# Moving one statistics instruction, a chunk's fusion and a norm's last step within the period of an attention-and-Mamba kernel

## The chip, the cores and the metric

The kernel runs on one core of a Trainium2 chip. The metric is the device time of one execution in microseconds, taken as the median of several runs. The engines are named as in the profile: PE (TensorE), DVE (VectorE), ACT (ScalarE), POOL (GpSimd) and SP (SyncE, which issues the DMAs). [...]

## The reference

The input x is 8 samples of 512 channels by 48 x 48 = 2304 positions. Two layers are applied, each with a residual:

```
x = x + attention(group_norm(x))      # causal linear attention, 8 heads of 64
x = x + mamba_groups(group_norm(x))   # 4 groups of 128 channels, one after the other
```

The attention projects q, k and v (512 x 512 each), takes elu + 1 of q and k, and forms for each position the causal sum of k v^T, read with q and divided by the running sum of k. The second layer splits the 512 channels in four. For each group i a Mamba block runs over the 2304 positions: in-projection, a causal convolution of width 4, silu, softplus of a step size, a scan h = dA * h + dBu with 256 channels x 16 states, a weighted sum over the states, a gate silu(z), an out-projection. Its output x_m is fused with its input x_i:

```
fused = sigmoid(mean(x_i)) * x_i + sigmoid(mean(max(x_i, x_m))) * max(x_i, x_m)
x_(i+1) = normed group i+1 + fused
```

so that a group's Mamba block needs the fusion of the group before. The group norms have 32 groups of 16 channels and use the mean and the variance over all positions.

## The kernel before, in words

Positions are cut into 6 chunks of LC = 384. A **job** is one chunk of one Mamba block: 192 jobs in all, of two interleaved streams (even and odd samples). A job is 8 **slots**. A slot multiplies and scans two pairs of states: one product on DVE (L809), a smaller one on POOL (L798), four exponentials dA = exp(delta * A) on ACT (L819, each into one of six PSUM banks), four scans on DVE (L830), one multiplication by C on POOL (L846), and four matmuls on PE that sum over the states (L853) into the bank `yp`. The exponentials are issued three ahead of the scans (DEPTH), five ahead just before silu and softplus (L670 and L704), because those two need another table on ACT and come back with a second table load.

Everything else is fitted in beside the slots. Each slot has two **halves**: `beside(2 * k)` is called before its first scan, `beside(2 * k + 1)` after its second. At each half a planner goes through its tasks and lets each one issue its next step once the step's due half is reached (`when[0]`), a least distance to its last step has passed (`when[1]`), and the banks that it wants are free. The tasks are written by hand as generators that yield their due halves:

- `chunk` (L266) computes one chunk of attention, started 16 halves after the one before it; its times are `at(j)`, j halves after its start. At `at(24)` DVE adds the attention's output to x (`xr`, L450), and `bn_stats` (L452) takes the chunk's statistics for the second layer's norm. After the sixth chunk `group_norm` (L162) makes the norm in five steps: aggregation and a matmul, three small DVE operations (L174 to L178), a second matmul, `pow` on POOL (L191, preceded by L188 on DVE), and two small DVE operations that use its result (L195).
- `prepare` (L623) makes a job's inputs before its first half `first`: convolution matmuls (L635) at first - 21 and first - 19, four silu on ACT (L671 to L676) at first - 18, then the step size, softplus (L706) four halves on, and the DMAs that spread rows over partitions.
- `pass_on` (L524) hands one block to the next: for each chunk c it loads three tiles by SP (L569, L572, L574), scales two or three of them on ACT (L596, L597 and L601, or L607 where a new sample starts), and adds on POOL (L604 and L609 one half apart, and L612 for the output). `self.ready` then lets the job's convolution start. Chunk 0 runs as soon as the block before is done; chunks 1 to 5 have due halves relative to their job's `first`.

In steady state `first` is a multiple of 16 and a chunk of attention starts 13 halves before it, so that everything repeats with a **period** of 16 halves, which holds one job and one chunk of attention. Below, "half n" is a half's number modulo 16, with half 0 at a job's first scan:

| step | half |
|---|---|
| attention output and its statistics (L450, L452) | 11 |
| convolutions (L635) | 11, 13 |
| silu (L671 to L676) | 14 |
| softplus (L706) | 2 |
| loads of a chunk's fusion, c = 1 to 5 | 12 |
| its scaling on ACT; its three additions on POOL | 2; 3, 4, 5 |
| scaling on ACT of chunk 0; its additions | 8; 9, 10, 11 |
| norm after a sixth chunk: five steps | 15, 0, 1, 2, 3 |
| exponentials for k on ACT (L298, L299); k on DVE (L351) | 6; 7 |

Of the kernel before, what the change touches and what calls it, by code (L numbers as in the profile page):

```python
# [49 lines left out]
def attention_then_mamba_kernel(  # L50
# [18 lines left out]
    B, _, L = x.shape  # L69
# [84 lines left out]
    def save(out, in_):  # L154
        stores.append((half_no[0], out, in_))

    def flush(every=True):
        while stores and (every or stores[0][0] <= half_no[0] - 2):
            _, o, i = stores.pop(0)
            nc.sync.dma_start(out=o, in_=i)  # L160
# [46 lines left out]
    norms, xns, x1s, done, ksums = {}, {}, {}, {}, {}  # L207
# [58 lines left out]
    def chunk(m):  # L266


        b, o, c = parts[m]
# [3 lines left out]
        cols, tile_rows = slice(c * LC, (c + 1) * LC), slice(o * P, (o + 1) * P)  # L273
# [6 lines left out]
        def new(tag, bufs=1, shape=(P, LC)):  # L280
            return apool.tile(list(shape), F32, tag=tag, name=f"{tag}_{n}", bufs=bufs)
# [50 lines left out]
        S, stats, ksum = passes[b, o]  # L332
# [90 lines left out]
        xr = new("xr")  # L423
# [25 lines left out]
        yield at(24), 0  # L449
        nc.vector.tensor_add(xr, xr, ops)  # L450
        bank.free()
        nc.vector.bn_stats(stats[:, 0, c, :], xr)  # L452
        save(x1s[b][tile_rows, cols], xr)
        if c + 1 == NC:
            norm = yield from group_norm(
                stats, 1, f"m{b}_{o}", 8, [(times[m] + j, 1) for j in (28, 29, 29, 30, 31)]
            )
            flush()
            done[b, o] = norm

    class Stream:
# [62 lines left out]
        def pass_on(self):  # L524


            xi = self.xi
            old = None
            if self.b is not None:
                old = self.b, self.s, self.n, self.fm  # L530
                wt = small.tile([P, 4], F32, tag="wt", name=f"wt_{self.n}")
                nc.vector.tensor_copy(wt[:, 2:3], self.sums)
                nc.vector.tensor_reduce(wt[:, 3:4], self.fsum, AX.X, ALU.add)
            last = old is not None and old[1] == 3 and not self.samples
            if not last:
                self.move_on()
                while (self.b, self.s) not in done:
                    yield "1w", 0
                norm = done[self.b, self.s]
            s = self.s  # L540
            if old is not None:
                yield "1", 0

                nc.scalar.activation(wt[:, 0:2], wt[:, 2:4], AF.Exp, scale=-1.0 / L)
                yield "1", 0
                nc.vector.tensor_scalar_add(wt[:, 0:2], wt[:, 0:2], 1.0)
                nc.vector.reciprocal(wt[:, 0:2], wt[:, 0:2])
            else:
                yield "1", 0
            if not last:  # L550
                if self.fresh:
                    self.sums = norm[:, 2, :]
                else:

                    sums = small.tile([P, 2], F32, tag="sums", name=f"sums_{self.n}", bufs=3)
                    nc.vector.tensor_scalar(
                        sums[:, 0:1], wt[:, 2:3], wt[:, 0:1], norm[:, 2, :], ALU.mult, ALU.add
                    )
                    nc.vector.tensor_scalar(
                        sums[:, 1:2], wt[:, 3:4], wt[:, 1:2], sums[:, 0:1], ALU.mult, ALU.add  # L560
                    )
                    self.sums = sums[:, 1:2]

            def loads(c):
                fu = xb = xa = None
                cols = slice(c * LC, (c + 1) * LC)
                if not last:
                    xb = mpool.tile([P, LC], F32, tag="xb", name=f"xb_{self.n}_{c}")
                    nc.sync.dma_start(out=xb, in_=x1s[self.b][s * P : (s + 1) * P, cols])  # L569
                if old is not None:  # L570
                    fu = mpool.tile([P, LC], F32, tag="fu", name=f"fu_{old[2]}_{c}")
                    nc.sync.dma_start(out=fu, in_=old[3][:, cols])  # L572
                    xa = mpool.tile([P, LC], F32, tag="xo", name=f"xo_{old[2]}_{c}")
                    nc.sync.dma_start(out=xa, in_=x1s[old[0]][old[1] * P : (old[1] + 1) * P, cols])  # L574
                return fu, xb, xa

            now = loads(0)
            for c in range(NC):

                if c and not last:  # L580
                    first = 2 * self.jobs[self.block * NC + c].start
                    yield (first - 36, 1), 0
                    now = loads(c)
                    yield (first - 30, 1), 0
                elif c:
                    yield "3", 0
                    now = loads(c)
                    yield "1", 0
                else:
                    yield "1", 0  # L590
                cols, icols = slice(c * LC, (c + 1) * LC), slice(3 + c * LC, 3 + (c + 1) * LC)
                fu, xb, xa = now
                if not last:
                    normed = dict(bias=norm[:, 1, :], scale=norm[:, 0, :])
                if old is not None:
                    nc.scalar.activation(fu, fu, AF.Copy, scale=wt[:, 1:2])  # L596
                    nc.scalar.activation(xi[:, icols], xi[:, icols], AF.Copy, scale=wt[:, 0:1])  # L597
                if old is None:
                    nc.scalar.activation(xi[:, icols], xb, AF.Identity, **normed)
                elif not last and not self.fresh:  # L600
                    nc.scalar.activation(xb, xb, AF.Identity, **normed)  # L601
                if old is not None:
                    yield "1", 0
                    nc.gpsimd.tensor_tensor(fu, fu, xi[:, icols], ALU.add)  # L604
                    yield "1", 0
                    if not last and self.fresh:
                        nc.scalar.activation(xi[:, icols], xb, AF.Identity, **normed)  # L607
                    elif not last:
                        nc.gpsimd.tensor_tensor(xi[:, icols], xb, fu, ALU.add)  # L609
                    self.ready = c + 1  # L610
                    yield "1", 0
                    nc.gpsimd.tensor_tensor(xa, xa, fu, ALU.add)  # L612
                    save(out[old[0], old[1] * P : (old[1] + 1) * P, cols], xa)
                self.ready = c + 1
# [335 lines left out]
    parts, times = [], []  # L950
# [17 lines left out]
    for b in counted:  # L968
        first = times[parts.index((b, 0, 0))]
        begins[b] = (first - 20) // PERIOD * PERIOD - 4 * NC * PERIOD - 2 if b > 1 else first - 64  # L970

    def begin(latest):

        nonlocal begun, put
        while counted and begins[counted[0]] - 4 <= half_no[0]:
            tasks.append(Task(statistics(counted.pop(0))))
        while put < len(parts) and times[put] - 6 <= half_no[0]:
            put += 1
            heads.append(Task(chunk(put - 1), before=heads[-1] if heads else None))
        while (  # L980
            begun < len(jobs)
            and jobs[begun].start <= latest
            and jobs[begun].stream.block == jobs[begun].block
            and jobs[begun].stream.ready > jobs[begun].c
        ):
            tasks.append(Task(jobs[begun].prepare(), jobs[begun].start))
            begun += 1
# [41 lines left out]
    def at(k):  # L1029
        return jobs[k // SLOTS], k % SLOTS  # L1030
# [170 lines left out]
```

## Time and profile before

| | us |
|---|---|
| median of 3 runs (lowest, highest) | 9154.76 (9140.69, 9157.51) |
| the profiled execution's own time | 9167.14 |
| its span, first to last instruction | 9165.3 |
| DVE busy | 8342.1 |
| POOL busy | 8066.8 |
| PE busy | 7631.5 |
| ACT busy | 6579.4 |

The span is divided by what the engines did; a share of busy time does not say by itself which engine sets the end. In the timelines shown below a line gives the start, the duration, the engine, the source line and operation, the tile written and read, and how many instructions are merged; in brackets stands the idle time of the engine before it and what ended it.

### The profile page before, as it was taken

The page shows a single profiled execution, that of the slowest core. Times are in us where ns is not written, and L with a number is a line of the kernel's source. Part 1 is how long each engine was busy: PE and PEld are TensorE (multiplying, and loading weights), DVE is VectorE, ACT ScalarE, POOL GpSimd, SP SyncE. Part 2 cuts the span into 40 slices and gives each one's busy share as a digit, 9 for nine tenths or more (in the row PEclk, how much of TensorE's full clock was granted, in tenths as well). Part 3 has the DMA queues.
Part 4 walks back from the last instruction along what each step waited for, and adds up shares of the span by engine and source line. Part 5 has one row for each costly group of instructions (what it writes and reads, how often), then busy time and mean ns, then how long its engine had stood idle before and what let it go on. Part 6 is the DMA issues. An engine that isn't in the chain of part 4 may idle for free.

```text
span 9165.3 us, 120476 instructions
## 1 busy us (share of the span) xinstructions
PE 7631.5 (83%) x35714; PEld 3602.8 (39%) x35714; DVE 8342.1 (91%) x11640; ACT 6579.4 (72%) x12656; POOL 8066.8 (88%) x5635
## 2 busy tenths in 40 slices
PE   7888888888888888888888888888888888888865
PEld 4443444433344444443333444444333444444321
DVE  3899999999999999999999999999999999999997
ACT  2677777777777777777777777777777777777775
POOL 1788989899988899899998888998999898989998
PEclk9999999999999999999999999999999999999977
DMA  5566666666766666666666666666666666666654
GB/s 182 161 173 180 185 184 184 181 188 180 196 173 179 184 186 187 183 180 181 191 184 182 174 178 187 187 184 184 180 188 183 181 179 177 178 178 177 164 156 129
DMA packets 1002898, 1642.84 MB, mean 179 GB/s; under 512 B 138592, under 2 KB 797312, under 8 KB 1002240
## 3 DMA queue, kind: packets, MB, share of 16 engines
q1 hardware_dynamic: 1002240, 1635.13, 65.0%
q8 instruction: 283, 4.64, 0.2%
q14 instruction: 375, 3.07, 0.1%
HBM read 1309.06 MB, written 325.58 MB: 178 GB/s over the span
## 4 chain that ended last, share of the span: by engine, by line
DVE 31%; ACT 21%; PE 18%; POOL 10%; DMA 9%; issue 8%; SPq 3%; POOLq 0%; DVEq 0%; ACTq 0%
DVE u L830 20%; ACT bank L819 7%; PE bank L635 6%; POOL u L846 6%; DVE u L809 6%; PE bank L286 5%; ACT L819 4%; PE yp L853 3%; PE bank L646 3%; POOL u L798 2%; DMA C<-scr 2%; ACT L706 2%; ACT bank L299 1%; DMA B<-scr 1%; SPq L739 1%
## 5 line engine op out<-in xcount | busy, mean ns | idle before, releaser
L830 DVE TENSOR_TENSOR_SCAN u<-bank,u 128x385 f32<-128x385 f32 (+1 forms) x6144 | 5471.0, 939 | 378.3 <-ACT bank L819 331.9
L846 POOL TENSOR_TENSOR u<-u,C 128x1536 f32<-128x1536 f32 x1536 | 4880.6, 3177 | 216.4 <-DVE gm_m L175 83.2
L819 ACT ACTIVATE bank<-dr,av 128x385 f32<-128x385 f32 (+1 forms) x6144 | 3432.3, 579 | 1406.9 <-DVE u L830 1118.1
L853 PE MATMUL yp<-u,cst 128*64 128x384 f32 x12288 | 2429.2, 516 | 505.7 <-ACT yp L787 263.9
L798 POOL TENSOR_TENSOR u<-B,dxr 128x512 f32<-128x512 f32 x1536 | 1958.8, 1275 | 21.4 <-DMA dxr<-xscr 16.9
L809 DVE TENSOR_TENSOR u<-B,dxp 128x1024 f32<-128x1024 f32 x1536 | 1835.0, 1195 | 9.4 <-ACT dxp L782 9.4
L286 PE MATMUL bank<-xn,wq_sb 128*128 128x384 f32 x4608 | 1730.3, 520 | 97.1 <-DVE u L830 40.4
L853 PEld LDWEIGHTS yp<-u,cst 128*64 128x64 f32 x12288 | 781.0, 139 | 1713.3 <-issue 1051.6
L635 PE MATMUL bank<-xi,wk 128*128 128x384 f32 x3072 | 1122.1, 509 | 306.1 <-ACT kl L383 234.3
L286 PEld LDWEIGHTS bank<-xn,wq_sb 128*128 128x128 f32 x4608 | 870.0, 199 | 894.6 <-DVE u L830 153.6
L635 PEld LDWEIGHTS bank<-xi,wk 128*128 128x128 f32 x3072 | 563.0, 193 | 878.2 <-ACT kl L383 351.5
L844 POOL COPY state<-u 128x4 f32<-128x4 f32 x1280 | 241.7, 189 | 538.4 <-DVE u L830 522.7
L298 ACT ACTIVATE ex<-bank,bqkv_sb 128x384 f32<-128x384 f32 x384 | 219.6, 572 | 520.1 <-PE bank L286 491.6
L747 POOL TENSOR_TENSOR delta<-delta,xs 128x384 f32<-128x384 f32 x384 | 384.6, 1002 | 141.6 <-DMA dscr<-delta 124.6
L819 ACT ACT_TABLE_LOAD x382 | 490.1, 1283 | 6.7
L787 ACT ACTIVATE yp<-xs,pv 128x384 f32<-128x384 f32 x384 | 222.7, 580 | 373.2 <-DVE yz L865 373.2
L871 PE MATMUL bank<-yz,wo 128*128 128x384 f32 x768 | 307.0, 517 | 55.5 <-DVE yz L865 36.7
L695 PE MATMUL bank<-dbc,wd 9*128 9x384 f32 x768 | 302.2, 513 | 3.2 <-ACT dbc L687 3.2
L646 PE MATMUL bank<-xi,wi 128*128 128x384 f32 x768 | 289.2, 498 | 14.3 <-ACT xs L671 14.3
L416 PE MATMUL bank<-cst,rdb 128*128 128x128 f32 x576 | 103.2, 290 | 228.3 <-DVE u L830 226.1
L447 PE MATMUL bank<-sm,v 128*64 128x128 f32 x2304 | 260.9, 305 | 33.8 <-DVE u L830 30.6
L682 PE MATMUL bank<-xs,wx 128*40 128x384 f32 x768 | 281.3, 489 | 0.8 <-DVE sm L434 0.8
(109 smaller groups left out, 7632.7 us busy)
## 6 DMA issues: line engine op xcount, KB each, us to landing
B<-scr SPq DMA_DIRECT2D x1536, 192.0 KB
C<-scr SPq DMA_DIRECT2D x1536, 192.0 KB
xn<-xn SPq DMA_DIRECT2D x192, 768.0 KB
dr<-dscr SPq DMA_DIRECT2D x768, 192.0 KB
dxr<-xscr SPq DMA_DIRECT2D x768, 192.0 KB
dscr<-delta SPq DMA_DIRECT2D x192, 384.0 KB
xscr<-delta SPq DMA_DIRECT2D x192, 384.0 KB
xn<-in_x SPq DMA_DIRECT2D x48, 768.0 KB
```

The costliest lines, as they stand in the source:

```text
L286: nc.tensor.matmul(ps, wq_sb[:, kt, j * 512 + o * P : j * 512 + (o + 1) * P], xn[:, kt, :], start=(kt == 0), stop=(kt == 3),)
L635: nc.tensor.matmul(xc, wk[:, k, h * P : (h + 1) * P], xi[:, c0 + k : c0 + k + LC], start=(k == 0), stop=(k == 3),)
L646: nc.tensor.matmul(zp, wi[:, 256 + h * P : 256 + (h + 1) * P], xi[:, c0 + 3 : c0 + 3 + LC], start=True, stop=True,)
L695: nc.tensor.matmul(vp, wd[32:41, h * P : (h + 1) * P], dbc[32:41, :], start=True, stop=True)
L747: nc.gpsimd.tensor_tensor(delta[:, h, :], delta[:, h, :], xs[:, h, :], ALU.mult)
L798: nc.gpsimd.tensor_tensor(u[:, :, :, 1 + LC - TAIL :], self.B[s % 4][:, :, cols].unsqueeze(2).to_broadcast(shape), self.dxr[s // 4][:, :, ...
L809: nc.vector.tensor_mul(u[:, :, :, 1 : 1 + LC - TAIL], self.B[s % 4][:, :, cols].unsqueeze(2).to_broadcast(shape), self.dxp.unsqueeze(1).to ...
L819: nc.scalar.activation(dA[:, cols], self.dr[h][:, g, cols], AF.Exp, scale=self.w[6][:, 2 * h + g, q + j : q + j + 1],)
L830: nc.vector.tensor_tensor_scan(u[:, j, g, cols], dA[:, cols], u[:, j, g, cols], 0.0, ALU.mult, ALU.add,)
L846: nc.gpsimd.tensor_tensor(h, h, self.C[s % 4].unsqueeze(2).to_broadcast([P, NG, 2, LC]), ALU.mult)
L853: nc.tensor.matmul(self.yp[g * 64 : g * 64 + 64, 0:LC], pair_sum, u[:, j, g, 1:], start=False, stop=(s % 4 == 3 and j == NG - 1), skip_gro ...
L871: nc.tensor.matmul(self.xm[:, 0:LC], self.w[2][:, h, :], self.yz[:, h, :], start=(h == 0), stop=(h == 1),)
```

## The change

Three steps are moved; no instruction is added or removed.

1. `bn_stats` on the attention's output leaves `at(24)` and gets a step of its own at `at(28)`: half 15 in place of half 11. The norm after a sixth chunk starts one half later than that.
2. The fusion of chunks 1 to 5 is loaded at first - 33 in place of first - 36 and scaled at first - 25 in place of first - 30; the additions follow one, two and three halves after the scaling as before. In halves: loads 12 to 15, ACT 2 to 7, POOL 3, 4, 5 to 8, 9, 10.
3. The due half of the norm's last step is 32 in place of 31. As each step is due at least one half after the one before, the five steps, which were issued at halves 15, 0, 1, 2, 3, are issued at 0, 1, 2, 3, 4.

```diff
         nc.vector.tensor_add(xr, xr, ops)
         bank.free()
+        save(x1s[b][tile_rows, cols], xr)
+        yield at(28), 0
         nc.vector.bn_stats(stats[:, 0, c, :], xr)
-        save(x1s[b][tile_rows, cols], xr)
         if c + 1 == NC:
             norm = yield from group_norm(
-                stats, 1, f"m{b}_{o}", 8, [(times[m] + j, 1) for j in (28, 29, 29, 30, 31)]
+                stats, 1, f"m{b}_{o}", 8, [(times[m] + j, 1) for j in (28, 29, 29, 30, 32)]
             )
...
                 if c and not last:
                     first = 2 * self.jobs[self.block * NC + c].start
-                    yield (first - 36, 1), 0
+                    yield (first - 33, 1), 0
                     now = loads(c)
-                    yield (first - 30, 1), 0
+                    yield (first - 25, 1), 0
                 elif c:
                     yield "3", 0
```

## Prediction

> **What bounds the kernel now.** I read the page first, then DVE's waits, then timelines of single periods.
>
> ```profile
> PE 7631.5 (83%) x35714; PEld 3602.8 (39%) x35714; DVE 8342.1 (91%) x11640; ACT 6579.4 (72%) x12656; POOL 8066.8 (88%) x5635
> L830 DVE TENSOR_TENSOR_SCAN u<-bank,u 128x385 f32<-128x385 f32 (+1 forms) x6144 | 5471.0, 939 | 378.3 <-ACT bank L819 331.9
> ```
>
> DVE is the busiest engine and its scans alone are 5471 us, so the end is set by DVE's work plus its waits, 9165 - 8342 = 823 us. The view of waits says for whom:
>
> ```profile
> DVE u L830 <- ACT bank L819: 331.9, 198, 4.4
> DVE k L351 <- ACT bank L299: 142.0, 135, 5.3
> DVE norm_m L195 <- POOL norm_m L191: 43.4, 31, 2.2
> DVE u L830 <- POOL state L844: 25.0, 70, 0.4
> ```
>
> (total us, times, longest.) I then gave each DVE wait in the timeline its half by counting scans, over the 174 periods of steady state: 270.3 us at half 15 (every period, 1.55 on average), 125.4 at half 7, 48.0 at half 3, 37.4 at half 4, 41 elsewhere. Everywhere else DVE runs without a gap. One period, DVE and then ACT:
>
> ```profile
> 4640.07 0.56 DVE L452 BATCH_NORM_STATS2 stats_m<-xr 128x6 f32<-128x384 f32 x1
> 4640.55 1.78 DVE L830 TENSOR_TENSOR_SCAN u<-bank,u 128x384 f32<-128x384 f32 x2
> ...
> 4651.64 0.95 DVE L830 TENSOR_TENSOR_SCAN u<-bank,u 128x384 f32<-128x384 f32 x1
> 4654.62 2.65 DVE L830 TENSOR_TENSOR_SCAN u<-bank,u 128x384 f32<-128x384 f32 x3 [2.04 <-ACT bank L819]
> ```
> ```profile
> 4649.33 1.28 ACT L671 ACT_TABLE_LOAD   x1
> ...
> 4652.71 1.28 ACT L819 ACT_TABLE_LOAD   x1
> 4654.01 1.09 ACT L819 ACTIVATE bank<-dr,av 128x384 f32<-128x384 f32 x2
> ```
>
> In silu's slot ACT makes no exponential from 4649.33 to 4654.01. DVE uses up the five in hand and stands for 2.04 us. The statistics run at half 11, back to back with scans, fully paid.
>
> The wait at half 7 has a chain behind it (ACT, PE, DVE of another period):
>
> ```profile
> 793.25 0.61 ACT L596 ACTIVATE fu<-fu,wt 128x384 f32<-128x384 f32 x1
> ...
> 794.28 0.69 ACT L601 ACTIVATE xb<-xb,norm_m 128x384 f32<-128x384 f32 x1
> ...
> 801.49 0.57 ACT L787 ACTIVATE yp<-xs,pv 128x384 f32<-128x384 f32 x1
> ```
> ```profile
> 802.21 2.10 PE L853 MATMUL yp<-u,cst 128*64 128x384 f32 x8 [1.99 <-ACT yp L787]
> 804.24 3.91 PE L286 MATMUL bank<-xn,wq_sb 128*128 128x384 f32 x8
> ```
> ```profile
> 809.24 0.55 DVE L351 SCALAR_TENSOR_TENSOR k<-ex,bank 128x384 f32<-128x384 f32 x1 [1.88 <-ACT bank L299]
> ```
>
> The fusion's three scalings stand in ACT's queue just ahead of softplus and its two table loads, and with no gap after them until L787. PE waits 1.99 us for L787, projects k late, and at half speed besides: the same eight matmuls take 2.85 us in a period 90 us earlier, and the granted clock from 804 to 809 is 0.76. ACT's exponential of k and DVE's L351 follow late.
>
> [...] the clock records show 47 episodes at 0.5 of 3.4 us each that begin in half 5. [...]
>
> **The change part by part.** The order of every other step's halves is as before; only the moved ones differ.
>
> *Statistics to half 15.* At half 11, L450 to the scan after L452 is 0.563 + 0.477 us from start to start; an addition followed directly by a scan is 0.46 (L372 to L830). Removal saves 0.58. At half 15 the instruction lies ahead of the waiting scan. ACT's chain there starts from a DVE scan at half 13 and does not depend on it. The trace already has this experiment, since the next sample's own statistics (L239, the same operation on the same shape) fall in this slot in some periods. Median wait with nothing added: 2.03 us (71 periods); with one at half 14: 1.57 (15); one at half 15: 1.35 (15); one at each: 1.07 (42). For example:
>
> ```profile
> 1109.59 0.55 DVE L239 BATCH_NORM_STATS2 stats_a<-xs 128x6 f32<-128x384 f32 x1
> ...
> 1112.12 2.66 DVE L830 TENSOR_TENSOR_SCAN u<-bank,u 128x385 f32<-128x385 f32 x3 [1.12 <-ACT bank L819]
> ```
>
> So it is free while more than about 0.5 us of wait is left, as in all but 3 of 174 periods. Gain 174 x 0.58 = 101 us; if the cover were gone, 174 x 0.1 = 17.
>
> *The norm one half later.* The aggregation (0.22 us to the next instruction) leaves half 15's cover: 29 x 0.22 = 6 lost. `pow` moves on POOL from between L846 and L798 to behind L798:
>
> ```profile
> 889.27 0.54 POOL L191 TENSOR_TENSOR norm_m<-gm_m,power 128x1 f32<-128x1 f32 x1
> 889.78 1.26 POOL L798 TENSOR_TENSOR u<-B,dxr 128x512 f32<-128x512 f32 x1
> ```
> ```profile
> 889.85 0.33 DVE L195 TENSOR_SCALAR norm_m<-gm_m,norm_m 128x1 f32<-128x1 f32 x2 [1.22 <-POOL norm_m L191]
> ```
>
> It will end 1.25 us later, near 891.05. L195 moves behind two scans, a product and the gate: 888.6 + 1.72 + 1.11 + 0.47 = 891.9. The wait disappears with 0.8 us to spare: 29 waits, 41 us; I take 38. The norm must be done by half 5, where `pass_on` asks for it; it is, at half 4.
>
> *The fusion.* ACT loses 0.52 + 0.51 + 0.60 = 1.63 us ahead of softplus. L787 comes at about 799.9, PE's idle time falls from 1.99 to about 0.2, the projection of k can start when L343 frees its bank (802.4) and ends at 805.2 in 2.85 us, L299 at 806.3; DVE wants it at 807.3, or 806.9 without its wait at half 4. Both waits go. The control is chunk 0, whose scaling is at half 8 already: over 29 such periods the wait is 0.0 at half 7 and 0.0 at half 4, against 0.3 to 1.3 and 0.2 to 0.3 in the other five kinds. (Those periods had a wait at half 3 too, which helped ACT catch up; hence not the full sum.) I take 113 of 125 and 33 of 37.
>
> Where the work lands: ACT at half 7 has waits for scans of 0.3 to 1.0 us between exponentials, and three exponentials are in hand; the next one that DVE wants is some 5 us off, the burst 1.63 plus 0.55. POOL from slot 4's start: L846 3.4, addition 1.0, L798 1.28, addition 1.0: `xi` is ready at 6.7 us, the convolution is due at 8.3. SP: the three loads pass the B rows of quarter 2 and C rows of quarter 0 (issued at 13, 14) and stand ahead of those of quarter 3; they have 8 halves to land, before 6, and the rows behind them four halves. The output's store moves with its addition, from half 7 to 12.
>
> What is late next: in a few periods POOL stands for up to 5.8 us for a DMA of delta before L747 (124.6 us in all). The additions now queue behind that wait. Some 8 such periods with c of 1 to 5, estimated 1.5 us each: 12 lost. In the 18 or so periods of a sample's first attention pass where POOL idles for only 1.25 to 1.5 us, part of the gain stays with POOL: 8 lost.
>
> Sum: -101 + 6 - 38 - 113 - 33 + 12 + 8 = -259 us. Against the profiled execution, 9165.3 of span in 9167.1 of time, that gives 8908; that execution was 12 us above the median shown, so I predict 9154.8 - 259 = 8896. With every term in full and nothing lost, 9154.8 - 304 = 8851.
>
> **The rivals.**
>
> *The half-7 wait stays.* PE's slow clock could come from its other gaps too (1.37 us in the same stretch), and a slow projection adds 1.06 us to 47 periods. For: 20 slow episodes start at half 2. Against: chunk 0. Without that term, 9154.8 - 146 = 9009.
>
> *The silu slot gives nothing.* If ACT's chain moves with DVE, the statistics cost as much there. For: PE's convolution at half 13 ends only 0.26 us ahead of the second silu. Against: L239. Then 9154.8 - 259 + 84 = 8980.
>
> *Slower: the fusion comes too late.* Where chunk 0's `xi` was ready 14.5 us after slot 4's start, silu began 4 us late and DVE stood 3.4 us more at half 14 and 2.1 at half 15: 5.5 in all, in 3 periods. Ready at 10.1 or 11.9 us it did no harm. For 6.7 to become 14 POOL must lag 7 us; it decides the sign from 259 / 5.5 = 47 of 160 fusions on. If all c of 1 to 5 in a first attention pass and half of the others did so (80), 9154.8 - 259 + 440 = 9336.
>
> **How the numbers follow.** The forecast, 0.70 (own range 8850 to 8950); the half-7 wait stays, 0.12; the slot gives nothing, 0.10; slower, 0.05; within 0.2%, 0.03. 0.2% (18 us) is about what a measurement of this kernel can tell from no change. The range 8835 to 9010 takes in the first three cases and drops the last two. Faster 0.92, same 0.03, slower 0.05.
>
> **What would show it.** Half 15's waits fall from 270 to about 175; L351's wait on L299 falls below 30, mostly outside steady state; L195's wait on POOL below 10; PE's slow episodes at half 5 vanish and the mean clock rises above 0.961. I am wrong if convolutions wait for L609 in chunks 1 to 5, if scans at halves 8 to 10 wait for ACT, or if L846 or L798 become releasers of scans.

## The result

| | us |
|---|---|
| after, median of 4 runs (lowest, highest) | 9042.0 (9038.1, 9045.5) |
| before, median of 4 runs beside them | 9151.35 (9140.7, 9157.5) |
| ratio, 95% interval | 0.9883 (0.9868 to 0.9897) |
| forecast, and its range | 8896 (8835 to 9010) |

The change gains 1.2%, where 2.8% was forecast; the time lies above the range. The profiled execution of after took 9045.5 us, with a span of 9043.8.

From the page of the kernel after, the busy times of the engines and the group of scans (lines from L454 on have moved down by one, so L831 is L830 of before, L820 is L819, and so on; the moved statistics are L454, where they were L452):

```profile
PE 7624.0 (84%) x35714; PEld 3639.7 (40%) x35714; DVE 8338.1 (92%) x11640; ACT 6578.6 (73%) x12656; POOL 8060.4 (89%) x5635
L831 DVE TENSOR_TENSOR_SCAN u<-bank,u 128x385 f32<-128x385 f32 (+1 forms) x6144 | 5466.5, 937 | 282.7 <-ACT bank L820 260.8
```

DVE's work is what it was (8342.1 before), so the gain lies in its waits. The view of DVE's waits of after gives, for each line and what it waited for, the total in us, the times and the longest:

```profile
DVE u L831 <- ACT bank L820: 260.8, 184, 4.6
DVE q L343 <- ACT bank L299: 130.6, 65, 6.0
DVE stats_a L239 <- DMA xs<-in_x: 56.0, 36, 4.0
...
DVE k L351 <- ACT bank L299: 30.0, 61, 4.8
DVE u L831 <- POOL u L799: 21.4, 21, 2.4
...
DVE norm_m L195 <- POOL norm_m L191: 8.8, 7, 2.2
```

Three lines fell as forecast: L351 from 142.0, the scans' wait for ACT from 331.9, L195 from 43.4. Three rose. Two of them the forecast had not named: L343, the q beside L351, and L239, the next sample's statistics. The third, the scans' wait for L799 (L798 of before), POOL's product, it had named as a sign of being wrong. In before these three were:

```profile
DVE q L343 <- ACT bank L299: 36.3, 16, 6.0
DVE stats_a L239 <- DMA xs<-in_x: 25.5, 14, 3.7
...
DVE u L830 <- POOL u L798: 8.2, 10, 1.4
```

By halves, over the same 174 periods of steady state, with the main kernels tried below (us):

| half | before | after | statistics alone | fusion alone | norm as before | weights behind | both repairs |
|---|---|---|---|---|---|---|---|
| 3 | 48.0 | 17.8 | 47.8 | 52.4 | 8.2 | 17.7 | 8.2 |
| 4 | 37.4 | 12.6 | 38.7 | 2.6 | 4.5 | 5.7 | 1.8 |
| 5 | 2.6 | 97.7 | 11.3 | 49.6 | 54.2 | 74.5 | 26.7 |
| 7 | 125.4 | 16.9 | 64.6 | 13.2 | 15.2 | 12.6 | 10.4 |
| 10 | 7.2 | 42.3 | 5.1 | 39.0 | 41.5 | 11.4 | 9.7 |
| 14 | 9.7 | 41.0 | 12.0 | 37.1 | 34.5 | 0.5 | 0.1 |
| 15 | 270.3 | 185.8 | 190.4 | 254.9 | 180.1 | 198.6 | 186.9 |

From before to after, halves 3, 4, 7 and 15 lose 248 us and halves 5, 10 and 14 get 162 back. So the gains came, nearly in full, and something new costs more than half of them.

The silu slot did what was forecast. DVE in the timeline of after, at half 15 of a period in which the next sample's statistics are here too:

```profile
3347.45 0.55 DVE L454 BATCH_NORM_STATS2 stats_m<-xr 128x6 f32<-128x384 f32 x1
3347.92 0.54 DVE L239 BATCH_NORM_STATS2 stats_a<-xs 128x6 f32<-128x384 f32 x1
...
3349.97 0.96 DVE L831 TENSOR_TENSOR_SCAN u<-bank,u 128x385 f32<-128x385 f32 x1 [0.65 <-ACT bank L820]
```

Two statistics stand ahead of the scan and 0.65 us of wait is still left: both are paid out of the wait.

### The first new wait: a bank behind softplus

The wait at half 5 has two owners, told apart by the chunk whose fusion runs in the period (29 periods of each kind): those of chunk 0 wait 1.62 us on average, those of chunk 3 1.32, the other four at most 0.27. Chunk 0's periods are those with the norm's steps. PE and then DVE of one of them, in the timeline of after:

```profile
3358.38 0.59 PE L186 MATMUL bank<-gm_m,cst 128*128 128x1 f32 x2 [3.65 <-ACT delta L707]
3358.90 2.83 PE L854 MATMUL yp<-u,cst 128*64 128x384 f32 x8
...
3362.35 3.31 PE L286 MATMUL bank<-xn,wq_sb 128*128 128x384 f32 x8
```
```profile
3366.76 0.55 DVE L343 SCALAR_TENSOR_TENSOR q<-ex,bank 128x384 f32<-128x384 f32 x1 [1.90 <-ACT bank L299]
```

L186 is the norm's second matmul, one column wide. One half later than before, the bank that is next in turn for it is one that softplus (L707) has yet to read. PE stands 3.65 us for ACT, until softplus has come behind its table load of 1.28 us and read the bank, and runs nothing else meanwhile. The sum over four matmuls (L854) and the projection of q (L286) behind it come late, and wholly or partly at half speed as well (the granted clock is 0.50 from 3358 to 3362 and 0.81 from there to 3366): 2.83 and 3.31 us, where the kernel with the norm as before, shown below, takes 1.51 and 2.85 at a clock of 1.00. The profile lists what PE waited for ahead of L186, in us and times; in after first, in before second:

```profile
  ACT delta L707: 237.5, 60
```
```profile
  DVE S L408: 15.8, 29
```

(60 waits in 30 of 32 norms: the weight load's and the matmul's are both counted, so that about half of the total is time that PE stood.) The clock records fit: before had 47 half-speed episodes that begin in half 5 and 20 in halves 2 and 3, 3.4 us each; after has none in half 5, and some 60 in halves 1 to 3, 28 of them beginning in half 2 and lasting 6.8 us. Its mean clock is 0.956 where before had 0.961.

### The second new wait: delta behind nine weight loads

Halves 10 and 14 wait almost only in the periods of chunk 2, 1.28 us each on average. In these, at half 4, the next block's weights are loaded, and SP issues them ahead of delta's store. SP, POOL and DVE of one of them, in the timeline of after:

```profile
3266.32 0.61 SPq L480 DMA_DIRECT2D wi<-in_win  x1
...
3276.02 0.38 SPq L716 DMA_DIRECT2D dscr<-delta  x1
...
3296.42 0.34 SPq L160 DMA_DIRECT2D out<-xo  x1
3296.81 0.43 SPq L246 DMA_DIRECT2D xs<-in_x  x1
```
```profile
3278.93 1.00 POOL L748 TENSOR_TENSOR delta<-delta,xs 128x384 f32<-128x384 f32 x1 [5.72 <-DMA dscr<-delta]
...
3288.85 1.00 POOL L605 TENSOR_TENSOR fu<-fu,xi 128x384 f32<-128x384 f32 x1
```
```profile
3299.56 0.56 DVE L239 BATCH_NORM_STATS2 stats_a<-xs 128x6 f32<-128x384 f32 x1 [3.07 <-DMA xs<-in_x]
```

The store goes out 9.7 us after the first weight load, and POOL stands 5.72 us for it. The fusion's additions now come behind that wait, so the output's store (L160), which needs the last of them, is issued only at 3296.42. SP has been standing for it since 3289.9, and the next sample's piece (L246) is queued behind it: L239, wanted at 3296.5, gets its data 3 us late. Waits of this kind are 31.6 us of the 41.0 at half 14.

At half 10 the same delay takes another way. Most of that half's wait, 26.8 of 42.3 us, lies in six of the 29 periods, those in which the block passed on starts a new sample. There ACT scales only after POOL's first addition (L608 behind L605), and its exponentials are queued behind that. ACT and DVE of one of them, in the timeline of after:

```profile
4678.60 0.71 ACT L608 ACTIVATE xi<-xb,norm_m 128x384 f32<-128x384 f32 x1 [8.89 <-POOL fu L605]
4679.21 2.08 ACT L820 ACTIVATE bank<-dr,av 128x385 f32<-128x385 f32 x4
```
```profile
4679.81 0.96 DVE L831 TENSOR_TENSOR_SCAN u<-bank,u 128x385 f32<-128x385 f32 x1 [4.58 <-ACT bank L820]
```

In before the periods of chunk 2 had their additions ahead of the wait, and they filled the time. POOL in the timeline of before:

```profile
3310.64 0.99 POOL L604 TENSOR_TENSOR fu<-fu,xi 128x384 f32<-128x384 f32 x1
...
3320.94 1.00 POOL L747 TENSOR_TENSOR delta<-delta,xs 128x384 f32<-128x384 f32 x1 [2.77 <-DMA dscr<-delta]
```

POOL does not catch up within the period. In the next one, chunk 3's, PE waits 1.37 and 1.61 us for L847 (up to 3307.04 and 3311.64), the granted clock is 0.79 from 3308 to 3316, and L343 waits again: that is the other half of half 5.

### The profile page after: what moved, and what is told of

It reads as the page before. It is cut to its first block, busy times and chain, and to the rows that moved or that the text cites. A ratio compares the mean times of both kernels' runs of the same rounds, so it can differ in the third digit from the quotient of the medians.

```text
span 9043.8 us, 120509 instructions
## 1 busy us (share of the span) xinstructions
PE 7624.0 (84%) x35714; PEld 3639.7 (40%) x35714; DVE 8338.1 (92%) x11640; ACT 6578.6 (73%) x12656; POOL 8060.4 (89%) x5635
## 4 chain that ended last, share of the span: by engine, by line
DVE 29%; POOL 21%; DMA 14%; ACT 11%; PE 11%; issue 8%; SPq 5%; POOLq 0%; DVEq 0%; ACTq 0%
DVE u L831 19%; POOL u L847 13%; DVE u L810 6%; ACT bank L820 4%; POOL u L799 4%; PE bank L636 4%; SPq L740 3%; PE bank L286 3%; DMA C<-scr 2%; DMA dscr<-delta 2%; PE yp L854 2%; ACT L820 2%; DMA B<-scr 2%; POOL delta L748 1%; ACT L707 1%
## 5 line engine op out<-in xcount | busy, mean ns | idle before, releaser
L831 DVE TENSOR_TENSOR_SCAN u<-bank,u 128x385 f32<-128x385 f32 (+1 forms) x6144 | 5466.5, 937 | 282.7 <-ACT bank L820 260.8
L847 POOL TENSOR_TENSOR u<-u,C 128x1536 f32<-128x1536 f32 x1536 | 4881.5, 3178 | 144.9 <-DVE u L831 34.9
L820 ACT ACTIVATE bank<-dr,av 128x385 f32<-128x385 f32 (+1 forms) x6144 | 3428.8, 579 | 1087.1 <-DVE u L831 817.4
L854 PE MATMUL yp<-u,cst 128*64 128x384 f32 x12288 | 2451.4, 521 | 409.4 <-POOL u L847 331.4
L799 POOL TENSOR_TENSOR u<-B,dxr 128x512 f32<-128x512 f32 x1536 | 1959.9, 1276 | 17.8 <-DMA dxr<-xscr 15.1
L286 PE MATMUL bank<-xn,wq_sb 128*128 128x384 f32 x4608 | 1685.1, 509 | 82.1 <-DVE u L831 27.4
L854 PEld LDWEIGHTS yp<-u,cst 128*64 128x64 f32 x12288 | 784.6, 140 | 1628.8 <-issue 812.9
L286 PEld LDWEIGHTS bank<-xn,wq_sb 128*128 128x128 f32 x4608 | 857.4, 197 | 829.1 <-DVE k L351 139.2
L443 PE MATMUL bank<-q,S 64*64 64x128 f32 x2176 | 243.9, 302 | 28.3 <-DVE u L831 27.9
```

Source lines behind the costliest of these rows:

```text
L286: nc.tensor.matmul(ps, wq_sb[:, kt, j * 512 + o * P : j * 512 + (o + 1) * P], xn[:, kt, :], start=(kt == 0), stop=(kt == 3),)
L799: nc.gpsimd.tensor_tensor(u[:, :, :, 1 + LC - TAIL :], self.B[s % 4][:, :, cols].unsqueeze(2).to_broadcast(shape), self.dxr[s // 4][:, :, ...
L820: nc.scalar.activation(dA[:, cols], self.dr[h][:, g, cols], AF.Exp, scale=self.w[6][:, 2 * h + g, q + j : q + j + 1],)
L831: nc.vector.tensor_tensor_scan(u[:, j, g, cols], dA[:, cols], u[:, j, g, cols], 0.0, ALU.mult, ALU.add,)
L847: nc.gpsimd.tensor_tensor(h, h, self.C[s % 4].unsqueeze(2).to_broadcast([P, NG, 2, LC]), ALU.mult)
L854: nc.tensor.matmul(self.yp[g * 64 : g * 64 + 64, 0:LC], pair_sum, u[:, j, g, 1:], start=False, stop=(s % 4 == 3 and j == NG - 1), skip_gro ...
```

## The experiments

Each ratio is against runs of before on the same chip, whose medians were 9158.6 for the kernels with the statistics alone, the fusion alone, the norm as before and the weights behind, and 9152.1 for the other four. Beside after it was 9151.35, so a difference in us between two kernels can be off by some 7 us where these medians differ.

**Each part alone.** First the statistics: moved to half 15 on the kernel before, with the norm's steps left at 15, 0, 1, 2, 3.

```diff
+        yield at(28), 0
         nc.vector.bn_stats(stats[:, 0, c, :], xr)
...
-                stats, 1, f"m{b}_{o}", 8, [(times[m] + j, 1) for j in (28, 29, 29, 30, 31)]
+                stats, 1, f"m{b}_{o}", 8, [(times[m] + 28, 0)] + [(times[m] + j, 1) for j in (29, 29, 30, 31)]
```

> The kernel before with the statistics alone moved to half 15; the norm's first step follows in the same half, so that its five steps stay at 15, 0, 1, 2, 3, and the fusion stays. If the wait in silu's slot covers the statistics as the next sample's statistics showed, 9151 - 101 = about 9050, half 15's waits fall from 270 to some 180 us and half 7 keeps its 125 us. If the slot gives no cover, about 9135 with half 15 at 270.

Measured: 9008.8 us, ratio 0.9840 (0.9824 to 0.9857). One of the change's parts alone is faster than the whole. Half 15 fell by 80 as expected, but the gain is 150 because half 7 fell too, from 125.4 to 64.6, which no theory had. PE's idle time ahead of the late projection is the same 1.99 us there, yet half-speed episodes at half 5 are 11 and not 47; the last section comes back to that.

Then the fusion's new halves alone, on the kernel before.

```diff
-                    yield (first - 36, 1), 0
+                    yield (first - 33, 1), 0
...
-                    yield (first - 30, 1), 0
+                    yield (first - 25, 1), 0
```

> The kernel before with the fusion's two due halves alone moved. Theory: the waits at halves 7 and 4 go (-108 and -37), but in the periods of chunks 2 and 3, where POOL starts the fusion late behind a DMA of delta, waits at halves 10, 14 and 5 appear that are worth about +100, so about 9110. Rival: the new waits belong to the norm's shift, the fusion keeps its whole gain, about 9005. L343 should wait in chunk 3's periods and not in chunk 0's by the theory.

Measured: 9086.4 us, ratio 0.9924 (0.9909 to 0.9939). Halves 4 and 7 fall to 2.6 and 13.2, and the second new wait appears in full, without the statistics: 39.0 at half 10, 37.1 at half 14, and 49.6 at half 5. Of that half-5 wait 42.3 us are in chunk 3's periods (1.46 us each). So the second wait belongs to the fusion. The first one is in neither of these two kernels (chunk 0's periods have 0.0 at half 5 in both), which leaves the norm. The time is some 24 us below what was expected.

**The norm as before, on the kernel after.** The first four steps go back to halves 15, 0, 1, 2; the last stays at 4, so that the power has its half more.

```diff
-                stats, 1, f"m{b}_{o}", 8, [(times[m] + j, 1) for j in (28, 29, 29, 30, 32)]
+                stats, 1, f"m{b}_{o}", 8, [(times[m] + 28, 0)] + [(times[m] + j, 1) for j in (29, 29, 30, 33)]
```

> The changed kernel with the norm's first step in the same half as the statistics and its last step due at 33: its five steps are issued at halves 15, 0, 1, 2 and 4. The second matmul at half 1 takes a bank that L408 freed, where at half 2 it takes the bank that softplus reads. Theory: that bank holds PE 3.65 us in chunk 0's periods, slows its clock and makes L343 wait; with it gone those 29 periods lose 2.2 us each, pow has its two halves, and the time is about 9042 - 65 = 8977. Rival: PE's late start comes from POOL, L343 waits in chunk 0's periods as before, about 9040 or slower, since L195 could wait again.

Measured: 8970.7 us, ratio 0.9796 (0.9781 to 0.9811), 71 below after. PE of the same kind of period, in this kernel's timeline:

```profile
3328.61 0.38 PE L186 MATMUL bank<-gm_m,cst 128*128 128x1 f32 x2
...
3332.81 2.85 PE L286 MATMUL bank<-xn,wq_sb 128*128 128x384 f32 x8 [0.24 <-DVE u L831]
```

L186 no longer waits, the projection is at full speed (the granted clock is 1.00 from 3325 to 3337), and L343 follows with no wait in this period. Chunk 0's periods fall from 1.62 us at half 5 to 0.04, and their mean length from 48.99 to 46.53 us: 29 x 2.46 = 71, the whole of the gain. Chunk 3's keep 1.39.

The late norm without the shared bank was tried too: the steps stay at 0, 1, 2, 3, 4 and the second matmul takes a column of the first one's bank, which is kept until then.

```diff
+        if n > 1:
             bank.free()
...
-        yield places[2], 1
-        var_ps = bank()
+        yield places[2], int(n > 1)
+        var_ps = bank() if n > 1 else mean_ps[:, 1:2]
```

> The changed kernel with the norm's steps at the same halves 0, 1, 2, 3, 4, but its second matmul written to a column of the bank that its first one holds, so that it takes no bank from softplus. Theory (the bank, not the half, is what holds PE): L343's wait in chunk 0's periods goes and the time is near that of the kernel with the norm early, 8965 to 8990. Rival (the half itself, or POOL): as the changed kernel, 9030 to 9045.

Measured: 8992.3 us, ratio 0.9830 (0.9814 to 0.9847), 50 below after and a little outside what was expected. Chunk 0's wait at half 5 is 0.0 at the old, late halves. So the cause is the bank, and not the norm's lateness. What it does not recover is at half 3: 49.4 us, of which the scans wait 41.2 for ACT in 29 periods, and the likely reason is that a bank held across softplus is one that the exponentials lack: in one such period ACT makes two exponentials after DVE's sum of S (L408) and before softplus' table load, where the kernel with the norm as before makes three.

**Delta's store ahead of the weights, on the kernel after.** Nothing but the order of two tasks on SP is changed.

```diff
-            if c == NC - 1 and (st.s < 3 or st.samples):
-                tasks.append(Task(st.weights()))
-
             def spread(what):
...
             dsrc = spread("dscr")
+
+            if c == NC - 1 and (st.s < 3 or st.samples):
+                tasks.append(Task(st.weights()))
```

> The changed kernel with the nine loads of the next block's weights issued behind the store of delta in place of ahead of it. Theory: these loads hold SP, delta's store comes late, POOL stands 5.7 us for it at half 5 in chunk 2's periods, and the fusion's additions queue behind; the output's store then holds SP at half 12. With it gone, waits at half 10 and 14 (74 us) and L343's in chunk 3's periods (38 us) mostly go: about 8950. Rival: POOL is late because it has too much to do, and the order on SP is not what counts: 9030 to 9045.

Measured: 8933.7 us, ratio 0.9756 (0.9741 to 0.9770), 108 below after, somewhat more than expected. SP and then POOL, in this kernel's timeline of the same kind of period (the store is L713 here):

```profile
3230.24 0.44 SPq L713 DMA_DIRECT2D dscr<-delta  x1
3230.77 0.51 SPq L480 DMA_DIRECT2D wi<-in_win  x1
```
```profile
3236.97 1.03 POOL L748 TENSOR_TENSOR delta<-delta,xs 128x384 f32<-128x384 f32 x1
```

POOL has no wait; its first addition follows 17.1 us after the store could go, in place of 22.5. SP still stands for the output's store (from 3248.4 to 3254.9), but the piece for L239 is issued at 3255.3, and L239 runs unhindered at 3260.2. In steady state half 10 falls from 42.3 to 11.4, half 14 from 41.0 to 0.5, and chunk 3's wait at half 5 from 1.32 to 0.44. From one period's first scan to the next one's, the periods of chunk 2 get shorter by 2.29 us on average and those of chunk 3 by 1.35: 29 x 3.64 = 106, nearly all that is gained here.

The same edit on the kernel before shows whether the order on SP was a cost of its own.

> The kernel before with the weights' loads behind delta's store and nothing else. Theory: there the fusion's additions fill POOL's wait, so little rests on it; the waits at halves 10 and 11 in chunk 2's periods (some 20 us) go: about 9130. Rival: the late store of delta costs the kernel before as much as the changed one, about 9045.

Measured: 9132.0 us, ratio 0.9978 (0.9971 to 0.9985). It is worth 20 there and 108 in after: the order had always been bad, and the additions had covered most of it.

**Both repairs.** Norm as before and weights behind, on the kernel after.

> The changed kernel with both repairs: the norm's steps at halves 15, 0, 1, 2, 4, and the weights' loads behind delta's store. Theory: the two costs lie in different periods (chunk 0's; chunk 2's and 3's) and add: 9042 - 71 - 108 = about 8863, with L343's wait at half 5 below 20 us. Rival: both come down to PE's slow clock and part of the gain was counted twice, 8900 to 8935.

Measured: 8859.9 us, ratio 0.9685 (0.9671 to 0.9700), faster than both kernels. The two gains add up: 71 + 108 = 179, and 182 is measured. (With each kernel counted from its own runs of before it is 79 + 116 = 195 and 183, so that this holds to some 12 us.) Half 5 keeps 26.7 us, where less than 20 was expected for L343, and no half but 15 has more.

**Both repairs, with the fusion at its old halves.** This takes the move of the fusion out of the best kernel.

```diff
-                    yield (first - 33, 1), 0
+                    yield (first - 36, 1), 0
...
-                    yield (first - 25, 1), 0
+                    yield (first - 30, 1), 0
```

> As the kernel with both repairs, but with the fusion at its old halves. Theory: the fusion's move is worth what its waits at halves 7 and 4 were with the statistics moved, 65 + 39 us, so about 8863 + 100 = 8965. Rival: without the norm's shift and the late store, PE's clock keeps out of the way by itself and the fusion's place hardly matters, within 20 us of the kernel with both repairs.

Measured: 8965.1 us, ratio 0.9796 (0.9782 to 0.9811), 105 slower than with the fusion moved. The wait that the move was forecast to remove comes back, in this kernel's view of waits:

```profile
DVE k L351 <- ACT bank L299: 108.4, 159, 5.8
```

It is 19.7 with both repairs; by halves, 94.3 at half 7 and 37.8 at half 4 against 10.4 and 1.8. That the 105 is so near the 100 expected is partly luck: half 7 was taken as 65 from the kernel with the statistics alone, and it came back as 94.3, with 25 half-speed episodes at half 5 where that kernel had 11, while some of the gain was lost at halves 5 and 10.

## Why the prediction was off

Step by step, in its own order:

- **Statistics to half 15: right.** Half 15 falls by 84.5 us, where 270 to about 175 was forecast; it ends at 185.8. Where only the statistics and no L239 stand in the slot, the median wait is 1.57 us, against 2.03 with nothing added before, a step of 0.46 us; L239 alone at half 14 had shown the same 1.57, and alone at half 15, 1.35. The rival that the slot gives nothing is out.
- **The fusion: the mechanism was right.** L351's wait is at 30.0 (forecast: below 30), half 7 at 16.9, half 4 at 12.6, and PE's slow episodes at half 5 are gone. So the rival that the half-7 wait stays falls too, though 9009 is the nearer number: the time got there by another way. In place, the move is worth 105 us and not 113 + 33: with the statistics moved, only 94.3 + 37.8 is there to remove, and a part of that comes back at halves 5 and 10. The two moves share the half-7 wait: each alone gains part of it, so that their gains can't be added up.
- **The norm one half later: this step failed.** The wait for the power did go, 43.4 to 8.8. But only `pow` and L195 were costed, two of five steps. The second matmul moves as well, and a matmul needs a bank; that its bank is next in turn behind softplus was not looked up, nor what is queued on PE behind it. A forecast of -38 + 6 hides a cost of 71.
- **What is late next: this step failed too.** It had the right wait (L747 on delta's DMA, up to 5.8 us) and the right danger (the additions queue behind it), and put it at "some 8 such periods", 1.5 us each. It is all 29 periods of chunk 2, at 2.6 us each, and then 1.3 in each of the 29 that follow. The order on SP costs 108 us in after and 20 in before, so 88 are new, where 12 was allowed. The estimate took the longest waits of the kernel before, some 8 of 33. The 28 in chunk 2's periods were 2.95 us on average, because three additions of 1 us each had just filled the rest; after has 28 of over 4 us in these periods, 5.6 on average. The question was not how long POOL stood, but how long it would stand with the additions taken out.

Put together: -259, with the bank's 71 and the 76 by which the other step was short, would be -112; -113 came against the median shown. With both repairs it is -292, of which the order on SP is worth 20 on its own (as on the kernel before); the other 272 answer to the forecast's -259 - 12 for a kernel in which nothing is late next. Both balances are arithmetic on medians that carry some 7 us from chip to chip, so that they close to 1 us is chance; and the sum's own half-7 term stood on a wait that differs from kernel to kernel with the slow episodes at half 5 (47, 11 and 25 of them), as the last section shows.

Of the signs named for being wrong, all three came. Scans at half 10 wait for ACT (31.9 us of the 42.3). L799, L798 of before, rose from 8.2 to 21.4 us as a releaser of scans. And convolutions stand for POOL's addition to `xi` (L610, L609 of before) in chunks 1 to 5 too: 48 times in steady state, 1.4 us on average, 21 of them in the periods of chunk 2, where before had this with chunk 0 alone. This third one seems to have done little harm: with both repairs 21 of these waits are left, and DVE's waits at half 14 are 0.1 us. The slower rival's 4 us at silu did not come; its idea, that the additions come too late behind POOL, was nearer to what happened than its place. The mean clock fell, from 0.961 to 0.956, where a rise was forecast. The sentence that DVE runs without a gap everywhere else passes over the 41 us listed just before it, about half of them at half 11.

The third step looks as if it gave the power a half more, but that isn't what it does. The last step's due half was already met by the least distance between steps, so 31 or 32 gives the same program, and `pow` is moved along with its reader. What ended the wait is that L195 moved behind two scans and a product, as forecast.

## What to carry to other kernels

When a step is moved, list everything it takes on the way, the bank and the queue too, and ask for each who had it last and what is queued behind: here a matmul of one column stopped PE for 3.65 us. Work that stands ahead of a wait is part of that wait's cover, so price a wait without it before moving it, and look at the order of issue in the DMA queue that feeds the wait, since that can cost nothing to mend. Two moves that draw on one wait should be tried apart: one of these alone beat the pair, though 61 us of its gain came at half 7 with fewer slow episodes, which nobody had aimed at, as the next section shows.

## What the runs showed of the hardware

PE gaps of the same 1.99 us at half 5 are followed by a half-speed episode in some periods and not in others. But for the last one of each trace, which begins some 10 us after the last scan, the slow episodes of before and of after are multiples of 3.413 us long, and the starts of one trace lie whole multiples of 3.4133 us apart, to within 0.03 us over the whole run. Counted in such steps from the first episode, the place where a gap begins goes with what follows. In steady state of before, of the gaps of over 1.5 us ahead of L853 at half 5 (1.69 to 2.11 us long), 59 begin in the first 1.7 us of a step, and 46 of these are followed by a slow episode; 47 begin later, and none is. In the kernel with the statistics alone the counts are 10 of 18 and 0 of 77; in before with the weights behind, 41 of 58 and 0 of 49; in both repairs with the fusion back, 25 of 33 and 0 of 74. This holds for the gaps at half 5: of all of PE's gaps of over 1.5 us in before, 98 are followed by a slow episode that starts with the next step, and 4 of these 98 begin later than 1.7 us in theirs.

It also goes with half 7's being better with the statistics moved. In before DVE waits 2.03 us at half 7 in the 46 periods with a slow episode at half 5 and 0.32 in the 60 that have the gap and no episode; with the statistics alone it is 1.99 in 11 periods and 0.33 in 85, as 77 of the gaps there began late in a step. The 35 episodes fewer, at 1.7 us each, are nearly all of the 61 us that half 7 lost. No run set on purpose where in a step a gap begins, so that its place decides is read from four traces and not tested.
